# Reading back the last expert steps of a graph-and-experts kernel step by step, with the last stores on SyncE and ScalarE

## The chip, the cores and the metric

The kernel runs on one core of one Trainium2 chip. The metric is the device time of one execution in microseconds; of several executions the median is given. The core has five engines with instruction streams of their own: TensorE (PE, matmuls; PEld are its weight loads), VectorE (DVE), ScalarE (ACT), GpSimd (POOL) and SyncE (SP). Each of them runs its stream in order; SP, ACT and POOL also issue DMA transfers, which the core's 16 DMA engines carry out.

## The reference

There are 6250 nodes with 256 features and 106250 edges (100000 and a loop at each node), sorted by their destination. The kernel computes two residual parts:

```python
deg = maximum(segment_sum(ones, dst), 1);  norm = deg ** -0.5
h = (norm * (layernorm(x) @ W.T + b))[src]
x = x + segment_sum(h, dst) * norm              # graph part
z = layernorm(x)
scores = z @ Wg.T + bg                          # 8 experts
top 2 of 8, probs = softmax of the two scores
x = x + sum over the two: prob * (relu(z @ W1[e].T + b1[e]) @ W2[e].T + b2[e])
```

The hidden width of an expert is 1024. Everything is float32.

## The kernel before

Nodes lie in 49 tiles of 128 (the last has 106 real ones); tile t of the residual is kept on chip as `g.xr[:, t, :]`. The graph part gathers source rows by 831 indirect DMAs of 128 edges each (`gather`, L463, on POOL) from a table in DRAM, and sums them with 0/1 masks on TensorE (L477). The edges don't fill the last of the 831 gathers: its last 118 are padding, with source 0.

As soon as a tile of nodes is summed, its two experts are chosen and its rows are sent to one queue for each expert in DRAM (`fhq`). The expert part works in 61 steps of 256 or 128 rows (`ROWS_OF`; the last three have 128, the six before them 256). `choose(step)` takes the longest queue, as many rows as the step has place for, and notes in `at` for each node and each of its two experts in which row of the result table the answer will be. `load_first`, `load_rows` and `load_second` bring weights and rows in from SP. `up` and `down` are the pieces of TensorE work, one piece each turn. A down sum of 128 rows is in a PSUM tile `py` (two buffers); `leave` (L836) adds the bias on DVE into `y` and writes it from SP to the result table `yq` in DRAM (`fyq`). Rows 0 to 127 of `yq` are zeros. `START[step]` is the first row of a step.

Results come back to the nodes by `read_back(t, j)` (L909): one indirect gather on POOL for tile t and choice j, a row of 256 float32 into each partition of a buffer `yb` (12 buffers). `add_in` (L918) multiplies it by the node's probability and adds it to `g.xr` on DVE. Before a tile is read, `results` (L904) makes integer rows `rowat` of `at`; a row that isn't below the bound becomes row 0. The table `DONE` says after which step which tiles are complete: (55, 42) means that tiles up to 41 are complete once step 55 has left, then (57, 43), (58, 44), (59, 48), and (60, 49) at the end. `bounds` holds the same for a check at the end of the run: if a row came later than `DONE` says, a flag `g.bad` sends the program into a slower general version (`any_order`), through a branch at L1508 that every engine passes.

The order of instructions is written out by hand. In the loop from L999 each turn s emits what is due: tasks planned for this turn (`plan_at`, `in_parts`), choosing and loading, one piece of TensorE work (`next_piece`), one gather at most (L1023), one add at most (L1027, `take`, at least eight turns after its gather unless the expert steps are over or many are pending), and a store of four complete tiles from POOL. A gather is held by semaphores until the results that it reads have landed; `free_order` says that it needn't wait for later steps. After the loop (L1033 to L1053) come tile 48's rows, the check for `g.bad`, the two gathers of tile 48, the store of tiles 44 to 47 from SP and that of tile 48 from ACT.

Of the kernel before, what the change touches and what calls it, by code (L numbers as in the profile page):

```python
# [7 lines left out]
F32 = mybir.dt.float32  # L8
BF16 = mybir.dt.bfloat16
F16 = mybir.dt.float16  # L10
I32 = mybir.dt.int32
# [60 lines left out]
        (52, 41), (55, 42), (57, 43), (58, 44), (59, 48), (USUAL - 1, NT))  # L72
LATER = 1 << 17
# [75 lines left out]
def in_order(ctx: ExitStack, tc: tile.TileContext, g: Shared):  # L149
# [698 lines left out]

    tasks = {}
# [59 lines left out]
    def read_back(pool, where, t, j, upto=USUAL - 1):  # L909
# [6 lines left out]
        return t, j, yb  # L916

    def add_in(t, j, yb):  # L918
        nc.vector.scalar_tensor_tensor(g.xr[:, t, :], yb, prob[:, t, j:j + 1], g.xr[:, t, :],  # L919
                                       op0=OP.mult, op1=OP.add)  # L920
# [35 lines left out]
    with tc.manual_schedule():  # L956
# [25 lines left out]
        with tc.tile_pool(name="ftail", bufs=2) as pool:  # L982
            s = NC
            pend = []
            plan = list(DONE)
# [4 lines left out]
            def take():  # L990
                nonlocal got, stored
                t, j, yb = pend.pop(0)[1]
                add_in(t, j, yb)
                got += 1
                if got == 2 * stored + 11:
                    store(stored, stored + 4, nc.gpsimd)
                    stored += 4

            while done < USUAL or tasks or len(plan) > 1 or asked < 2 * allowed or pend:  # L999
                for fn, args in tasks.pop(s, []):  # L1000
                    fn(*args)
                if s > all_sent and s > max(STREAM)[0] + 6:
                    if chosen < min(USUAL, upped + 4):
                        run(choose(chosen))
                        chosen += 1
                    if loaded2 < min(loaded1, gone + 3):
# [10 lines left out]
                if len(plan) > 1 and done > plan[0][0] and s >= since.get(plan[0][0], 0) + 6 \  # L1017
# [8 lines left out]

                if pend and (gone == USUAL or len(pend) > 10 or s >= pend[0][0] + 8):  # L1027
                    take()
                s += 1

            results(allowed, NT, float(START[USUAL]))  # L1033
            late = work.tile([P, NT, 2], F32, name="late", bufs=1)
            missed = work.tile([P, 2], F32, name="missed")
            nc.vector.tensor_tensor(late, at, bounds, op=OP.is_ge)
            nc.vector.tensor_reduce(missed[:, 0:1], late, op=OP.add, axis=mybir.AxisListType.XY)
            nc.vector.tensor_reduce(missed[:, 1:2], most, op=OP.max, axis=mybir.AxisListType.X)
            nc.vector.tensor_scalar(missed[:, 1:2], missed[:, 1:2], float(SLOTS), None, op0=OP.is_gt)
            nc.vector.tensor_add(missed[:, 0:1], missed[:, 0:1], missed[:, 1:2])  # L1040
# [512 lines left out]
```

## Time and profile before

| | |
|---|---|
| time, median of 3 runs | 1559.64 us (1556.26 to 1563.23) |
| the profiled execution's own time | 1577.23 us |
| its span, first to last instruction | 1575.4 us |
| mean granted TensorE clock | 0.933 |
| busy: PE, DVE, POOL, ACT | 1257.4, 981.8, 905.4, 398.5 us |
| last edge gather begins (L463) | 1334.4 us |
| last piece of a down sum ends | 1553.6 us |
| last gather of results begins (L911) | 1564.7 us |
| last store issued (L928, from ACT) | 1568.8 us |

The times inside a profiled execution are those of that one execution, from its first instruction on. In the lists of the profile a line has start, duration, engine, line of the code, operation, names (written<-read), count, and in brackets how long the engine had been idle and what ended that. "issue" is time in which the engine waited for nothing that the profile shows. fyq is the result table, yb a gathered buffer, y a result on its way out.

### The profile page before, as it was taken

The numbers are of one execution on the slowest core, as the hardware profiler recorded it, in microseconds if no ns is written. First come the engines' busy times: TensorE is split into PE (matmuls) and PEld (weight loads), VectorE is DVE, ScalarE is ACT, GpSimd is POOL, SyncE is SP. The second block draws the span as 40 slices with busy tenths as digits, with TensorE's granted clock in tenths as the row PEclk, the third lists the DMA queues.
The fourth block names the chain that finished last, engine by engine and source line by source line (L and its number), as shares of the span: only waits on it lengthen the run. The fifth ranks groups of instructions, "written<-read, shape, count | busy, mean of one in ns | idle before, by whom it ended". The sixth has DMA issues, their size and how long they took to land.

```text
span 1575.4 us, 24788 instructions
## 1 busy us (share of the span) xinstructions
PE 1257.4 (80%) x6562; PEld 942.8 (60%) x6562; DVE 981.8 (62%) x5472; ACT 398.5 (25%) x949; POOL 905.4 (57%) x976
## 2 busy tenths in 40 slices
PE   5348778798889879888988887888888888867994
PEld 5225456466656656666656565666656666655773
DVE  8712665657666666776766666767756665674632
ACT  3502222122232222322222222222222222221221
POOL 3166666666566656665656656666666665236633
PEclk9968988999999989999989999999999999987997
DMA  7633385677666676766676767766767866668873
GB/s 231 208 94 90 107 289 164 187 238 231 196 209 217 209 242 214 238 196 232 209 238 186 242 193 229 213 220 219 266 219 216 273 201 222 220 209 330 292 258 119
DMA packets 160927, 337.38 MB, mean 214 GB/s; under 512 B 26900, under 2 KB 106344, under 8 KB 145160
## 3 DMA queue, kind: packets, MB, share of 16 engines
q1 hardware_dynamic: 114348, 207.57, 38.1%
q0 software_dynamic: 46176, 127.59, 28.5%
q8 instruction: 54, 0.88, 0.2%
q14 instruction: 97, 0.79, 0.2%
q10 hardware_dynamic: 252, 0.53, 0.1%
HBM read 280.44 MB, written 55.16 MB: 213 GB/s over the span
## 4 chain that ended last, share of the span: by engine, by line
PE 62%; DVE 16%; issue 9%; another core or an unknown queue 5%; DMA 4%; ACT 2%; SPq 2%; POOL 0%; ACTq 0%; DVEq 0%; POOLq 0%
PE ph L818 23%; PE py L828 18%; PE ps L477 10%; PE pt L570 3%; PE ph L520 2%; PE ps L980 2%; PE px L702 1%; PE count L295 1%; DVE mask L470 1%; SPq L725 1%; DMA w<-in_W 1%; DVE scr L754 1%; ACT hid L820 1%; DMA xT<-fhq 1%
## 5 line engine op out<-in xcount | busy, mean ns | idle before, releaser
L463 POOL DMA_INDIRECT rows<-ftable,src x831 | 789.7, 950 | 506.5 <-issue 176.5
L818 PE MATMUL ph<-xT,w 128*128 128x256 f32 (+1 forms) x1952 | 513.4, 390 | 121.1 <-issue 72.6
L818 PEld LDWEIGHTS ph<-xT,w 128*128 128x128 f32 x1952 | 363.4, 200 | 243.0 <-issue 125.2
L828 PE MATMUL py<-w,hid 128*128 128x256 f32 x1760 | 462.2, 388 | 0.8 <-ACT hid L820 0.7
L820 ACT ACTIVATE hid<-ph,w 128x256 f32<-128x256 f32 (+1 forms) x488 | 216.9, 452 | 790.2 <-PE ps L477 226.5
L828 PEld LDWEIGHTS py<-w,hid 128*128 128x128 f32 x1760 | 336.5, 194 | 77.0 <-issue 4.5
L477 PE MATMUL ps<-rows,mask 128*128 128x512 f16 x831 | 320.6, 394 | 38.4 <-DMA rows<-ftable,src 26.9
L470 DVE TENSOR_SCALAR mask<-col_b,rel 128x128 f16<-128x128 bf16 x831 | 199.5, 266 | 28.7 <-remote 18.0
L911 POOL DMA_INDIRECT yb<-fyq,rowat x98 | 95.0, 970 | 108.2 <-DMA fyq<-y 52.5
L840 DVE TENSOR_TENSOR y<-py,w 128x256 f32<-128x256 f32 x110 | 46.4, 422 | 156.2 <-PE py L828 64.2
L477 PEld LDWEIGHTS <-mask 128*128 128x128 f16 x831 | 84.7, 103 | 70.1 <-issue 26.8
L577 DVE SCALAR_TENSOR_TENSOR xr<-pt,norm,xr 128x256 f32<-128x256 f32 x49 | 23.7, 483 | 119.0 <-PE ps L477 56.1
L537 DVE SCALAR_TENSOR_TENSOR rolled<-rolled,keep,ps 128x256 f32<-128x256 f32 x149 | 70.7, 475 | 35.9 <-PE ps L477 18.7
L552 ACT ACTIVATE whole<-rolled 32x256 f32<-32x256 f32 (+2 forms) x156 | 63.9, 410 | 63.8 <-DVE rolled L537 20.4
L570 PE MATMUL pt<-gw,uT 128*128 128x264 f32 x196 | 54.9, 404 | 20.0 <-issue 11.1
L540 DVE TENSOR_TENSOR rolled<-ps,rolled 128x256 f32<-128x256 f32 x150 | 63.7, 424 | 10.4 <-DVE rolled L537 2.9
L520 PE MATMUL ph<-wg,turned 128*128 128x8 f32 x196 | 30.9, 285 | 48.2 <-ACT turned L512 36.2
L520 PEld LDWEIGHTS ph<-wg,turned 128*128 128x128 f32 x196 | 30.1, 231 | 57.1 <-ACT turned L512 41.8
L919 DVE SCALAR_TENSOR_TENSOR xr<-yb,prob,xr 128x256 f32<-128x256 f32 x98 | 46.1, 482 | 28.3 <-DMA yb<-fyq,rowat 19.1
L570 PEld LDWEIGHTS pt<-gw,uT 128*128 128x128 f32 x196 | 36.8, 194 | 34.9 <-issue 15.1
L702 PE MATMUL px<-slots,h2s 128*128 128x256 f16 x196 | 30.6, 280 | 33.0 <-DVE slots L689 10.6
L980 PE MATMUL ps<-nothing 128*128 128x512 f16 x162 | 49.8, 426 | 0.0
(187 smaller groups left out, 1152.8 us busy)
## 6 DMA issues: line engine op xcount, KB each, us to landing
w<-in_W SPq DMA_DIRECT2D x61, 1152.0 KB
w<-in_W SPq DMA_DIRECT2D x61, 1028.0 KB
fhq<-ordered SPq DMA_DIRECT2D x392, 64.0 KB
fyq<-y SPq DMA_DIRECT2D x110, 128.0 KB
rows<-ftable,src POOLq DMA_INDIRECT x831
xT<-fhq SPq DMA_DIRECT2D x49, 256.0 KB
out<-xr POOLq DMA_DIRECT2D x11, 512.0 KB
xr<-in_x SPq DMA_DIRECT2D x6, 896.0 KB
```

What stands on the lines that cost most here:

```text
L463: nc.gpsimd.indirect_dma_start(out=rows[c], out_offset=None, in_=table[:, :], in_offset=bass.IndirectOffsetOnAxis(ap=g.src[:, c:c + 1], ax ...
L470: nc.vector.tensor_scalar(masks[c], g.col_b[:, r:r + P], g.rel[:, c:c + 1], None, op0=OP.is_equal)
L477: nc.tensor.matmul(sums[w], masks.pop(c), rows.pop(c), start=(c == chunks[0]), stop=(c == chunks[-1]))
L520: nc.tensor.matmul(px[:, t - t0], xT[:, k, (t - t0) * P:(t - t0 + 1) * P], wg[:, k, :], start=(k == 0), stop=(k == 1))
L537: nc.vector.scalar_tensor_tensor(new, rolled, keeps[kept[w]], ps[:, 0:D], op0=OP.mult, op1=OP.add)
L552: nc.scalar.activation(whole[t][p0:p1, :], new[p0:p1, :], AF.Copy)
L570: nc.tensor.matmul(pl, uT[:, k, :], gw[:, k, :], start=(k == 0), stop=(k == 1))
L818: nc.tensor.matmul(ph[:, :n], w1[:, k * H + b * P:k * H + (b + 1) * P], f["xT"][:, :n, k], start=(k == 0), stop=(k == 1))
L820: nc.scalar.activation(f["hid"][:, b, :n], ph[:, :n], AF.Relu, bias=w1[:, 2 * H + b:2 * H + b + 1])
L828: nc.tensor.matmul(f["py"], f["hid"][:, b, a * P:(a + 1) * P], f["w2"][:, b * D:(b + 1) * D], start=(b == 0), stop=(b == HB - 1))
L911: r = nc.gpsimd.indirect_dma_start(out=yb, out_offset=None, in_=yq[0:START[upto + 1], :], in_offset=bass.IndirectOffsetOnAxis(ap=where[:, ...
L980: nc.tensor.matmul(sums[WINDOW[s]], nothing[:, 0:P], nothing, start=False, stop=False)
```

## The change

Tiles 42 to 48 are no longer read only when they are complete. `WHOLE` reads them, two gathers for each tile, once step 56 has left, with everything that the steps up to 56 have given. For steps 57 to 60, `own_of` works out for each node of the open tiles the row that this one step has for it (row 0 where there is none; a node has at most one row in a step) and the probability that goes with it, and `read_own` gathers it: one gather for a tile and step, for the tiles that are still open at that step (`OWN`). The adds of both kinds go through `take`. The check for `g.bad` becomes `verdict`, spread over turns after step 60 has been chosen. POOL stores tiles in fours only up to tile 39; from there stores come from ACT or SP, in the last turns. Nothing is left behind the loop.

```diff
--- before.py
+++ after.py
@@ -70,6 +70,9 @@
 
 DONE = ((36, 26), (38, 28), (40, 29), (41, 30), (42, 31), (43, 32), (46, 35), (49, 37), (50, 38), (51, 39),
         (52, 41), (55, 42), (57, 43), (58, 44), (59, 48), (USUAL - 1, NT))
+OWN = {USUAL - 1 - i: max(t for step, t in DONE if step < USUAL - 1 - i) for i in range(4)}
+SPLIT = min(OWN)
+WHOLE = [d for d in DONE if d[0] < SPLIT - 1] + [(SPLIT - 1, NT)]
 LATER = 1 << 17
 TURNED, PLACED, SORTED, SENT = 5, 17, 22, 24
 LEAD = (13, 12)
@@ -846,6 +849,57 @@
             gone += 1
 
 
+    own_row, own_share = {}, {}
+
+    def own_of(step, pool):
+
+        t0 = OWN[step]
+        lo, n = START[step], NT - t0
+        here = pool.tile([P, n, 2], F32, name="here")
+        nc.vector.tensor_scalar(here, at[:, t0:, :], float(lo + ROWS_OF[step]), None, op0=OP.is_lt)
+        nc.vector.scalar_tensor_tensor(here, at[:, t0:, :], float(lo), here, op0=OP.is_ge, op1=OP.mult)
+        yield
+        place = pool.tile([P, n, 2], F32, name="place")
+        nc.vector.tensor_mul(place, at[:, t0:, :], here)
+        own_row[step] = pool.tile([P, n], I32, name="row", bufs=4)
+        nc.vector.tensor_add(own_row[step], place[:, :, 0], place[:, :, 1])
+        yield
+        nc.vector.tensor_mul(here, here, prob[:, t0:, :])
+        own_share[step] = pool.tile([P, n], F32, name="share", bufs=4)
+        nc.vector.tensor_add(own_share[step], here[:, :, 0], here[:, :, 1])
+
+    def read_own(pool, step, t):
+        i = t - OWN[step]
+        yb = pool.tile([P, D], F32, name="yb", bufs=12)
+        r = nc.gpsimd.indirect_dma_start(
+            out=yb, out_offset=None, in_=yq[0:START[step + 1], :],
+            in_offset=bass.IndirectOffsetOnAxis(ap=own_row[step][:, i:i + 1], axis=0))
+        free_order(r, [w for of, w in writes if of > step], "rows of later steps aren't read")
+        reads.append(r)
+        return t, own_share[step][:, i:i + 1], yb, step
+
+    def verdict():
+
+        late = work.tile([P, NT, 2], F32, name="late", bufs=1)
+        missed = work.tile([P, 2], F32, name="missed")
+        nc.vector.tensor_tensor(late, at, bounds, op=OP.is_ge)
+        nc.vector.tensor_reduce(missed[:, 0:1], late, op=OP.add, axis=mybir.AxisListType.XY)
+        yield
+        nc.vector.tensor_reduce(missed[:, 1:2], most, op=OP.max, axis=mybir.AxisListType.X)
+        nc.vector.tensor_scalar(missed[:, 1:2], missed[:, 1:2], float(SLOTS), None, op0=OP.is_gt)
+        yield
+        nc.vector.tensor_add(missed[:, 0:1], missed[:, 0:1], missed[:, 1:2])
+        nc.vector.tensor_add(missed[:, 0:1], missed[:, 0:1], g.outside)
+        ones = work.tile([P, 1], F32, name="ones")
+        nc.vector.memset(ones, 1.0)
+        yield
+        yield
+        pm = psp.tile([1, 1], F32, name="pt", bufs=1)
+        nc.tensor.matmul(pm, missed[:, 0:1], ones, start=True, stop=True)
+        yield
+        yield
+        nc.vector.tensor_scalar(g.bad, pm, 1.0, None, op0=OP.min)
+
     tasks = {}
 
     def plan_at(s, fn, *args):
@@ -913,10 +967,10 @@
             in_offset=bass.IndirectOffsetOnAxis(ap=where[:, t, j:j + 1], axis=0))
         free_order(r, [w for step, w in writes if step > upto], "rows of later steps aren't read")
         reads.append(r)
-        return t, j, yb
-
-    def add_in(t, j, yb):
-        nc.vector.scalar_tensor_tensor(g.xr[:, t, :], yb, prob[:, t, j:j + 1], g.xr[:, t, :],
+        return t, prob[:, t, j:j + 1], yb, None
+
+    def add_in(t, share, yb):
+        nc.vector.scalar_tensor_tensor(g.xr[:, t, :], yb, share, g.xr[:, t, :],
                                        op0=OP.mult, op1=OP.add)
 
     def store(t0, t1, engine=None):
@@ -982,27 +1036,39 @@
         with tc.tile_pool(name="ftail", bufs=2) as pool:
             s = NC
             pend = []
-            plan = list(DONE)
+            plan = list(WHOLE)
+            own = [(step, t) for step in sorted(OWN) for t in range(OWN[step], NT)]
+            ready = OWN[SPLIT]
             got = asked = allowed = stored = 0
             latest = 0
             since = {}
 
             def take():
-                nonlocal got, stored
-                t, j, yb = pend.pop(0)[1]
-                add_in(t, j, yb)
+                nonlocal got, stored, ready
+                t, share, yb, step = pend.pop(0)[1]
+                add_in(t, share, yb)
                 got += 1
-                if got == 2 * stored + 11:
-                    store(stored, stored + 4, nc.gpsimd)
-                    stored += 4
-
-            while done < USUAL or tasks or len(plan) > 1 or asked < 2 * allowed or pend:
+                if step is None:
+                    if got == 2 * stored + 11 and stored + 4 <= OWN[SPLIT]:
+                        store(stored, stored + 4, nc.gpsimd)
+                        stored += 4
+                elif OWN.get(step + 1, NT) > t:
+                    ready += 1
+                    if t == NT - 1 or gone == USUAL and ready % 2 == 0:
+                        store(stored, t + 1, nc.scalar if t % 4 < 2 else nc.sync)
+                        stored = t + 1
+
+            while done < USUAL or tasks or plan or own or asked < 2 * allowed or pend:
                 for fn, args in tasks.pop(s, []):
                     fn(*args)
                 if s > all_sent and s > max(STREAM)[0] + 6:
                     if chosen < min(USUAL, upped + 4):
                         run(choose(chosen))
+                        if chosen in OWN:
+                            in_parts(s + 1, own_of, chosen, pool)
                         chosen += 1
+                        if chosen == USUAL:
+                            in_parts(s + 4, verdict)
                     if loaded2 < min(loaded1, gone + 3):
                         load_second(loaded2)
                         loaded2 += 1
@@ -1014,7 +1080,7 @@
                 next_piece(s)
                 if done > over:
                     since[over] = s
-                if len(plan) > 1 and done > plan[0][0] and s >= since.get(plan[0][0], 0) + 6 \
+                if plan and done > plan[0][0] and s >= since.get(plan[0][0], 0) + 6 \
                         and asked == 2 * allowed:
                     step, t1 = plan.pop(0)
                     results(allowed, t1, float(START[step + 1]))
@@ -1024,33 +1090,13 @@
                     pend.append((s, read_back(pool, rowat, asked // 2, asked % 2, latest)))
                     asked += 1
 
+                elif own and asked == 2 * NT and done > own[0][0] and s >= since[own[0][0]] + 2 \
+                        and (s % 4 or done == USUAL):
+                    pend.append((s, read_own(pool, *own.pop(0))))
+
                 if pend and (gone == USUAL or len(pend) > 10 or s >= pend[0][0] + 8):
                     take()
                 s += 1
-
-
-
-            results(allowed, NT, float(START[USUAL]))
-            late = work.tile([P, NT, 2], F32, name="late", bufs=1)
-            missed = work.tile([P, 2], F32, name="missed")
-            nc.vector.tensor_tensor(late, at, bounds, op=OP.is_ge)
-            nc.vector.tensor_reduce(missed[:, 0:1], late, op=OP.add, axis=mybir.AxisListType.XY)
-            nc.vector.tensor_reduce(missed[:, 1:2], most, op=OP.max, axis=mybir.AxisListType.X)
-            nc.vector.tensor_scalar(missed[:, 1:2], missed[:, 1:2], float(SLOTS), None, op0=OP.is_gt)
-            nc.vector.tensor_add(missed[:, 0:1], missed[:, 0:1], missed[:, 1:2])
-            nc.vector.tensor_add(missed[:, 0:1], missed[:, 0:1], g.outside)
-            ones = work.tile([P, 1], F32, name="ones")
-            nc.vector.memset(ones, 1.0)
-            pm = psp.tile([1, 1], F32, name="pt", bufs=1)
-            nc.tensor.matmul(pm, missed[:, 0:1], ones, start=True, stop=True)
-            nc.vector.tensor_scalar(g.bad, pm, 1.0, None, op0=OP.min)
-            last = [read_back(pool, rowat, t, j) for t in range(allowed, NT) for j in range(2)]
-            if stored < allowed:
-                store(stored, allowed, nc.sync)
-            for t, j, yb in last:
-                add_in(t, j, yb)
-                if j:
-                    store(t, t + 1, nc.sync if t % 2 else nc.scalar)
 
 
 @with_exitstack
```

## Prediction

> **What bounds the kernel now.** I read the page first, then the chain of waits over the last 75 us, then the timelines of POOL and DVE there, and last two narrow DMA windows for a cost that the tail of before does not show.
>
> From the page, the span, the slices of POOL and two groups:
>
> ```profile
> span 1575.4 us, 24788 instructions
> ...
> POOL 3166666666566656665656656666666665236633
> ...
> L911 POOL DMA_INDIRECT yb<-fyq,rowat x98 | 95.0, 970 | 108.2 <-DMA fyq<-y 52.5
> ...
> L919 DVE SCALAR_TENSOR_TENSOR xr<-yb,prob,xr 128x256 f32<-128x256 f32 x98 | 46.1, 482 | 28.3 <-DMA yb<-fyq,rowat 19.1
> ```
>
> TensorE bounds nearly everything up to about 1553 us, and the change leaves that part alone. What it touches is the read-back of expert results: 98 gathers on POOL, whose idle time ahead of them ended mostly with the landing of a result (fyq<-y). The last slices of POOL are loose (2, 3, 6, 6, 3, 3): it has room, but, as will be seen, not much.
>
> The end of the chain of waits (start, us, what):
>
> ```profile
> 1547.34 0.43 DVE y L840
> ...
> 1547.79 1.68 DMA fyq<-y
> ...
> 1550.23 0.95 POOL yb L911
> 1551.18 0.30 issue
> 1551.49 0.94 POOL yb L911
> ...
> 1563.44 4.25 DMA yb<-fyq,rowat
> ...
> 1568.24 0.48 DVE xr L919
> ```
>
> See how the bound changes hands. TensorE ends at 1553.5, but the chain does not run through the last step's result. It runs through step 59's (y at 1547.34), then through eight gathers one after another on POOL (tiles 44 to 47, two each), then the adds, and only then the two gathers of tile 48 and the last store. One gather costs POOL 0.95 us and 0.30 us of issue.
>
> POOL's own timeline shows the room that exists:
>
> ```profile
> 1518.03 0.80 POOL L926 DMA_DIRECT2D out<-xr  x1
> 1537.39 0.97 POOL L911 DMA_INDIRECT yb<-fyq,rowat  x1 [18.57 <-DMA fyq<-y]
> 1538.66 0.95 POOL L911 DMA_INDIRECT yb<-fyq,rowat  x1 [0.30 <-issue]
> ...
> 1556.17 0.82 POOL L926 DMA_DIRECT2D out<-xr  x1
> ...
> 1564.69 0.95 POOL L911 DMA_INDIRECT yb<-fyq,rowat  x1 [0.30 <-issue]
> ```
>
> And DVE's gives the times at which each step's result leaves:
>
> ```profile
> 1523.43 0.42 DVE L840 TENSOR_TENSOR y<-py,w 128x256 f32<-128x256 f32 x1
> ...
> 1553.61 0.42 DVE L840 TENSOR_TENSOR y<-py,w 128x256 f32<-128x256 f32 x1 [4.86 <-PE py L828]
> ```
>
> These two are the second half of step 56 and all of step 60. The last half of step 57 leaves at 1534.42, step 58 at 1539.69, step 59 at 1547.34.
>
> **The change, part by part.** *Number of gathers.* The new constants come out as SPLIT = 57 and OWN = 57:42, 58:43, 59:44, 60:48. Tiles 0 to 41 are read as before: 84 gathers. Then, once step 56 is done, tiles 42 to 48 are read for everything up to it: 7 x 2 = 14 gathers. Then step 57 is read for 7 tiles, 58 for 6, 59 for 5, 60 for one: 19. The total is 117 where it was 98. After the one store on POOL at 1518.03, before issues 14 gathers and a store; after must issue 33 gathers.
>
> *When POOL can begin.* Step 57's result left DVE at 1534.42 and its gather began at 1537.39: 2.97 us. Step 59 took 1547.34 to 1550.23: 2.89. So step 56, at 1523.43, can be gathered from about 1526.4. By the loop's counters the results row for it is asked six slots after the step ends (a slot being one piece of TensorE work, some 0.66 us here), while its landing is still under way, so the order in the program doesn't hold it back.
>
> *How long POOL needs.* The gathers from 1550.23 to 1555.23 stand 1.25 us apart; the group's mean of 970 ns with 0.30 of issue is 1.27. I take 1.26. The 33rd starts 32 x 1.26 = 40.3 us after the first: 1566.7. Before, the last started at 1564.69. The 18.57 us hole and the smaller ones (3.4, 5.0 and 2.7 us) are used up by 19 x 1.26 = 23.9 us of added work, less the store (0.82 + 0.30) that leaves POOL. Everything POOL waits for is then there already: step 57 needed 1537.4 and is asked at 1526.4 + 14 x 1.26 = 1544.0; step 58 at 1552.9 against 1542.7; step 59 at 1560.4 against 1550.2; step 60 at 1566.7 against 1556.6.
>
> *What the moved adds do to DVE.* There are 19 more adds of 0.48 us; DVE was busy 4 us between 1524 and 1550, so they fit. But DVE runs in order, and by the loop's counters the result of step 59 now stands behind 17 of the new adds, that of step 60 behind 24. The 17th gather starts at 1546.6; with 2.7 us to land (1559.82 plus 2.70 in the chain) and one add it is 1549.8, so step 59's result leaves 2.4 us late. The 24th gives 1558.6, so step 60's is 5.0 us late and can be gathered from 1561.5. POOL wants it at 1566.7: hidden, with 5 us to spare. TensorE doesn't stall on that: step 60's sum uses the PSUM buffer that step 58 freed at 1540.
>
> *Choosing rows and the verdict.* own_of adds seven small DVE operations for each of four steps, 28 x about 0.16 us (row of L763: 0.17) = 4.5 us, in parts between the pieces of steps 54 to 56. The verdict (about 1.2 us of DVE, one tiny matmul) moves from the end to the same place. DVE is busy 10.7 us of 20 between 1500 and 1520, so I take zero. Without that cover the matmul would stand in TensorE's stream waiting for DVE, at most about 1 us, and step 56 and the whole POOL chain would shift by it. The verdict was not on the old chain either: its operations ran while the last gathers flew.
>
> *Stores.* Tiles 40 to 43 leave POOL's queue and go out with 44 and 45 in one 768 KB store from ACT, then 256 KB from SP, then tile 48 from ACT. ACT's and SP's queues hold nothing else by then. Before, 512 KB stood in that place, and the gather issued just after it took 4.25 us to land against 2.70 elsewhere. I therefore give the last gather 4.25.
>
> *Rows that aren't there.* This is the cost that the tail does not show. Each partition gathers one row, and where its row is not in the step asked for it reads the zero row 0. Step 57 has at most 256 true rows over 7 x 128 reads, 58 has 128 over 768, 59 has 128 over 640: at least 640, 640 and 512 repeats, about 100 of 128 in each gather. The nearest row is the last edge gather (L463 at 1334.38): it carries the 118 padding edges, which all read row 0. Its data, beside an ordinary gather of the same 128 KB (columns: PE, PEld, DVE, ACT, POOL, clock, DMA share, GB/s):
>
> ```profile
> 1336.00:1337.70 1.70, 1.43 (x8) 0.89 (x7) 1.59 (x13) 0.47 (x1) 0.00 (x0) 1.00 0.57 77
> 1544.60:1545.40 0.80, 0.80 (x8) 0.74 (x7) 0.00 (x0) 0.25 (x1) 0.60 (x1) 1.00 0.57 164
> 25.00:26.00 1.00, 1.00 (x33) 1.00 (x33) 1.00 (x8) 0.99 (x2) 0.00 (x0) 1.00 0.34 109
> ```
>
> It took 1.7 us instead of 0.8, longer than the 1.26 at which POOL sends gathers. The third line is the bias gbs, 128 reads of one row by an ordinary DMA: 109 GB/s, which is 1.2 us per 128 KB. If gathers in a row overlap their slow ends, the engines keep pace and the backlog is 0; if each costs 1.7 us alone, it is 19 x 0.44 = 8.4 us. I take 1.5 us, nearer the lower end because ramps and slow ends of neighbours can overlap, and keep both.
>
> *A rule against the row.* The Trainium skill, "DMA: Bandwidth & Descriptors", section "Anatomy of one DMA — SWDGE (gpsimd) path", gives each POOL-issued DMA about 2.0 us fixed plus bytes / 436e3: 2.3 us for 128 KB. If each gather paid that in turn, 19 more would cost 44 us and the end would move by some 30. The trace has them 1.25 us apart while each needs about 2.7 us to land, so the fixed part overlaps with the next; I use the row.
>
> *Sum.* 1566.7 + 4.25 landing + 1.5 backlog + 0.5 for one add (before had two) = 1573.0, where before its last store was issued at 1568.75. The 6.65 us from there to the end stay. That is +4.2 us on the profiled execution of 1577.23 us (span 1575.4 and 1.8 around it). It is 1.1% above the median of 1559.64; I carry the difference over as it is: 1564.
>
> **The rivals.** *First, the gain arrives.* If POOL were not the limit, step 60's gather would start at 1556.6 and the store at 1556.6 + 3.5 + 0.5 = 1560.6, 8.1 us earlier: 1551.5. For it: behind step 60 there is one gather where there were two, and these no longer wait for the adds of tiles 44 to 47. Against it: 33 gathers between 1526.4 and 1556.6 need a pace of 0.94 us, which is the bare 0.95 without any issue time, and no pair in POOL's timeline is that close.
>
> *Second, the repeated row decides: slower.* From 1544 on the 16 DMA engines, not POOL, set the pace. Its price is 19 x 0.44 = 8.4 us in place of my 1.5, so about +11: 1571. It counts as slower from an own gather of 1.5 us upward (19 x 0.27 = 5.1 with the 2.7 of the rest gives 7.8). For it: the 1.7 us row, and that last steps may be less than full, which makes still more repeats. Against it: 109 GB/s on the broadcast load.
>
> *Third, POOL simply changes places with the wait:* the forecast itself without a backlog, +2.7: 1562.3.
>
> **How the numbers follow.** 0.5% (7.8 us) is about what a measurement of this kernel can tell from no change. The likeliest case (POOL full, backlog small) I give 0.64, within 0.5%, its own range 1558 to 1567. The repeated row deciding, with anything else that makes the new wait longer (a late verdict, the larger stores), gets 0.32 and is slower. The gain gets 0.04. The range takes the likeliest case down to 1557 (a pace of 1.2 saves 2 us, the runs shown spread by 3.5 either way) and up into the second rival: 1573.
>
> **What would show it.** Right: 117 gathers; POOL without a hole over 1 us from 1526 to the last gather; that gather starting near 1566.7 of the same clock; the chain at the end running through POOL's gathers of steps 56 to 60; step 59's and 60's y late on DVE without a TensorE stall. A gather-to-add time growing from 2.7 us to over 6 along the own gathers would show the second rival. A last gather that starts when step 60 lands, with POOL idle ahead of it, would show the first and prove me wrong; so would gathers closer than 1.2 us.

## The result and the profile after

The changed kernel took 1574.17 us (median of 6 runs, 1571.01 to 1579.58) against 1560.51 us for the kernel before (6 runs): a ratio of 1.0096, 95% interval 1.0072 to 1.0120. It is 13.7 us slower. Forecast were +4.2 us, and a range that ended at 1573.

The two profiled spans, 1575.4 and 1576.6 us, differ by 1.2 us only, because in the profiled execution of before the part up to step 56 happened to be 15 us later. Count from step 56's last y (DVE) to the end of the span instead: before 1575.4 - 1523.43 = 52.0 us, after 1576.6 - 1508.16 = 68.4 us. The tail is 16.4 us longer, and that is where the change sits. All tails below are counted like this.

The page of after (lines moved by 3 in the main part: y is now L843, the old gather L965, the new one L874):

```profile
span 1576.6 us, 24873 instructions
...
POOL 2166666666666656666666666666666663355753
...
L965 POOL DMA_INDIRECT yb<-fyq,rowat x98 | 94.5, 964 | 87.6 <-DVE mine L771 27.8
```

98 gathers as before and 19 new ones (a smaller group). POOL's last slices (5, 5, 7, 5, 3) don't tell where in the tail it stood, since one slice is 39 us long. Its timeline does (start, us, engine, line, operation, idle before and what ended it):

```profile
1511.86 0.97 POOL L965 DMA_INDIRECT yb<-fyq,rowat  x1 [7.59 <-DMA fyq<-y]
...
1535.74 0.95 POOL L874 DMA_INDIRECT yb<-fyq,row  x1 [0.30 <-issue]
1543.16 1.07 POOL L874 DMA_INDIRECT yb<-fyq,row  x1 [6.47 <-DVE xr L973]
...
1555.84 0.95 POOL L874 DMA_INDIRECT yb<-fyq,row  x1 [3.49 <-DMA fyq<-y]
...
1563.54 0.95 POOL L874 DMA_INDIRECT yb<-fyq,row  x1 [1.63 <-DVE xr L973]
```

The first 20 gathers run 1.25 us apart, as worked out. Then POOL stands: for a free buffer (an add, xr), and for step 60's result (fyq<-y). From the first of the 33 gathers to the last it is 51.7 us instead of 40.3. DVE's timeline says what came late:

```profile
1508.16 0.42 DVE L843 TENSOR_TENSOR y<-py,w 128x256 f32<-128x256 f32 x1 [1.28 <-PE py L831]
...
1521.09 0.42 DVE L843 TENSOR_TENSOR y<-py,w 128x256 f32<-128x256 f32 x1 [1.24 <-issue]
1542.07 0.42 DVE L843 TENSOR_TENSOR y<-py,w 128x256 f32<-128x256 f32 x1 [17.69 <-PE py L831]
```

These are step 56's last y, step 57's second half and step 58. In the kernel before, step 57's second half and step 58 stand so:

```profile
1534.42 0.42 DVE L840 TENSOR_TENSOR y<-py,w 128x256 f32<-128x256 f32 x1 [4.84 <-PE py L828]
1539.69 0.42 DVE L840 TENSOR_TENSOR y<-py,w 128x256 f32<-128x256 f32 x1 [4.78 <-PE py L828]
```

Step 58's y comes 21 us after step 57's second half; before, it came 5.3 us after it. DVE waited for TensorE. And the chain of waits (start, us, what) runs through TensorE, where it stands still twice:

```profile
1521.75 5.41 issue
1527.15 1.22 PE ph L821 x4
1528.37 1.71 PE py L831 x4
1530.08 9.03 issue
1539.11 1.22 PE ph L821 x4
...
1563.54 5.65 DMA yb<-fyq,row
```

"issue" means that the profile shows nothing that TensorE waited for. But each of the two matmul groups needs the PSUM buffer that a relu on ScalarE frees, and ScalarE's timeline has these just ahead:

```profile
1526.73 0.37 ACT L823 ACTIVATE hid<-ph,w 128x128 f32<-128x128 f32 x1 [7.41 <-remote]
...
1538.68 0.37 ACT L823 ACTIVATE hid<-ph,w 128x128 f32<-128x128 f32 x1 [11.58 <-remote]
```

In the kernel before, ScalarE waits about 0.95 us at this place:

```profile
1537.51 0.37 ACT L820 ACTIVATE hid<-ph,w 128x128 f32<-128x128 f32 x1 [0.90 <-PE ph L818]
```

So TensorE waits for ScalarE, and ScalarE for TensorE's signal that a sum in PSUM is complete. "remote" means that the signal arrived just then and no instruction ended near it. The matmuls in question are these:

```profile
1518.95 0.62 PE L821 MATMUL ph<-xT,w 128*128 128x128 f32 x4
...
1520.27 0.62 PE L821 MATMUL ph<-xT,w 128*128 128x128 f32 x4
```

Their ends are modelled by the profile, but the groups behind them in TensorE's order started at 1519.41 and 1520.72, and another at 1527.15. In the trace's list of semaphore updates (from which some are missing) TensorE's next counts after 1516.95 are stamped 1526.71 and 1538.61. By these starts TensorE was past the work; its signal came some 7 and 18 us after the modelled ends. The second release comes 2 us after POOL's unbroken run of gathers ends at 1536.69.

### The profile page after: what moved, and what is told of

It is laid out like the page before. It is cut to its first block, busy times and chain, and to the rows that moved or that the text cites. A ratio compares the mean times of both kernels' runs of the same rounds, so it can differ in the third digit from the quotient of the medians.

```text
span 1576.6 us, 24873 instructions
## 1 busy us (share of the span) xinstructions
PE 1258.2 (80%) x6562; PEld 946.7 (60%) x6562; DVE 988.9 (63%) x5512; ACT 399.7 (25%) x949; POOL 924.4 (59%) x994
## 4 chain that ended last, share of the span: by engine, by line
PE 31%; DVE 11%; issue 6%; another core or an unknown queue 3%; DMA 3%; SPq 1%; ACT 1%; POOL 0%; ACTq 0%; POOLq 0%; DVEq 0%
PE ph L821 12%; PE py L831 12%; PE ps L480 5%; PE pt L573 1%; DMA xT<-fhq 1%; DVE scr L757 1%; PE px L705 1%; SPq L728 1%; DVE mask L473 1%; ACT hid L823 1%; DVE xr L973 1%; DMA fhq<-ordered 0%; DVE rolled L540 0%; DVE y L843 0%
## 5 line engine op out<-in xcount | busy, mean ns | idle before, releaser
L965 POOL DMA_INDIRECT yb<-fyq,rowat x98 | 94.5, 964 | 87.6 <-DVE mine L771 27.8
L843 DVE TENSOR_TENSOR y<-py,w 128x256 f32<-128x256 f32 x110 | 46.4, 421 | 140.6 <-PE py L831 69.6
L540 DVE SCALAR_TENSOR_TENSOR rolled<-rolled,keep,ps 128x256 f32<-128x256 f32 x149 | 70.7, 474 | 28.8 <-remote 13.7
L705 PEld LDWEIGHTS <-h2s 128*128 128x128 f16 x196 | 19.8, 101 | 51.3 <-issue 41.0
```

Source lines behind the costliest of these rows:

```text
L540: nc.vector.scalar_tensor_tensor(new, rolled, keeps[kept[w]], ps[:, 0:D], op0=OP.mult, op1=OP.add)
L705: nc.tensor.matmul(r.px[:, k, :], h2s[r.t][:, i, k * P:(k + 1) * P], slots[r.t], start=(i == 0), stop=(i == 1))
L965: r = nc.gpsimd.indirect_dma_start(out=yb, out_offset=None, in_=yq[0:START[upto + 1], :], in_offset=bass.IndirectOffsetOnAxis(ap=where[:, ...
```

## Experiments

Times differ between the sessions in which kernels ran together, so each is given as a ratio to runs of the kernel before on the same chip in the same session.

### The repeated row, and the buffers

The forecast's rival was the zero row that most partitions of a new gather read. In the first run each partition's missing row is a zero row of its own (the edit in short):

```
-        own_row[step] = place[:, :, 0] + place[:, :, 1]
+        own_row[step] = max(place[:, :, 0] + place[:, :, 1], g.pid)      # the same for rowat
```

> The changed kernel, but a node that has no row in the steps asked for reads zero row p of the result table (p its partition; rows 0 to 127 are all zeros) instead of row 0: one more small DVE operation (max with the partition number) for each list of rows. As many gathers, in the same order, with the same sums. Theory A (the repeated row is what costs: gathers of one row hold the DMA engines, and ACT and TensorE stand still behind them): the 9 us and 5 us holes of TensorE after step 57 vanish or shrink below 3 us in all, the last gather is some 42 us after step 56 has left instead of 55, and the time falls from 1.0096 of before to 0.997 to 1.003. Theory B (19 more gathers on POOL and the adds queued in front of y on DVE are what costs, whatever they read): the time stays at 1.007 to 1.012.

Measured: 1599.64 against 1583.47 us, 1.0109 (1.0066 to 1.0152); tail 68.1 us. The last landing took 4.11 us instead of 5.65, but the two late signals are there as before, with ScalarE waits of 6.80 and 12.33 us. By these two profiles the repeated row costs 1.5 us once, the value taken in the forecast, and it isn't the cause of the rest.

The second variant has 24 instead of 12 buffers yb, so that POOL need not wait for adds:

```
-        yb = pool.tile([P, D], F32, name="yb", bufs=12)
+        yb = pool.tile([P, D], F32, name="yb", bufs=24)
```

> The changed kernel with 24 instead of 12 buffers yb, so that POOL doesn't wait for adds that stand behind a late y on DVE (its hole of 6.5 us). If the chain POOL waits for DVE waits for TensorE is what lengthens the end, POOL's hole goes and the time falls by about 6 us (to about 1.006 of before); if DMA is what limits (theory A), gathers are issued earlier but land no earlier: within 0.2% of the changed kernel's 1.0096.

Measured: 1610.40 us, 1.0177 (1.0133 to 1.0220), worse than the change itself. The tail, 70.3 us, is no shorter: POOL's run now has 21 gathers and ends at 1569.38, and ScalarE is free at 1573.16. The rest of the loss lies ahead of the tail, since the edit gives the earlier gathers more buffers too: from the first gather of results to step 56's last y it is 174.1 us, where the run before this one took 164.5, and POOL's longest unbroken run there has 27 DMAs instead of 22. The lack of buffers is not what holds the kernel up. It only ends POOL's run earlier.

### Gathers that nobody reads, in the kernel before

Nineteen gathers more in the kernel before, after step 57, in three turns of four, into buffers that nothing reads. In the first all partitions read row 0, in the second partition p reads row p:

```
+            more, spare = 19, pool.tile([P, 1], I32, name="spare", bufs=1)
+            nc.vector.tensor_scalar(spare, g.pid, 0.0, None, op0=OP.mult)      # 1.0 in the second
...
+                if more and done > 57 and s % 4:
+                    nothing_back = pool.tile([P, D], F32, name="nb", bufs=12)
+                    nc.gpsimd.indirect_dma_start(out=nothing_back, ..., in_=yq[0:P, :], in_offset=spare)
+                    more -= 1
```

> The kernel before with 19 gathers more, emitted from the turn after step 57 on, three turns in four; all 128 partitions read row 0, into buffers that nothing reads. They wait for no result, so POOL has room for most of them in the hole that it had from 1518 to 1537. Theory A: they slow the landing of weights, results and rows around them; stands of ACT and TensorE appear while they fly, and the time rises by 0.5% or more (8 us and up). Theory B: POOL only fills its hole, a few of the 19 push the gathers of tiles 42 to 47 back by 0 to 6 us; the time rises by at most 0.3%, the same as with 19 different rows.

> As the run with 19 gathers of row 0 more, but partition p reads row p: the same number, size and places, no repeats. Theory A: near the time of before (0.998 to 1.003), and clearly below the run with repeats. Theory B: the same time as the run with repeats.

Measured: 1.0103 (1.0059 to 1.0146) and 1.0086 (1.0053 to 1.0119); tails of 71.0 and 67.6 us. Neither the adds nor the choosing of rows nor the stores of the change are in these kernels, and a cost of the same size is there. ScalarE's waits in the tail of the second (us in total, times, longest):

```profile
ACT hid L820 <- remote: 18.0, 3, 7.4
```

### What it is about a gather

Four ways to have a part of a gather. POOL busy without any transfer (19 memsets of the same length); the transfers without POOL (19 plain loads of 128 KB from SP); gathers of a quarter of the data; and full gathers scattered over steps 41 on.

```
+                    nothing_set = pool.tile([P, 1250], F16, name="nb", bufs=2)       # POOL alone
+                    nc.gpsimd.memset(nothing_set, 0.0)
...
+                    nc.sync.dma_start(nothing_back, yq[0:P, :])                      # transfers alone
...
+                    nc.gpsimd.indirect_dma_start(out=nothing_back[:, 0:64], ...)     # rows of 256 bytes
...
+                if more and done > 40 and s % 16 == 0:                               # scattered
```

> Part changed: 19 memsets of a 128x1250 f16 tile that nobody reads (by the 0.51 us of the 128x512 memset some 1.25 us each, the pace of the gathers) stand on POOL where the run of 19 cold gathers stood, after step 57; no transfer is added. In the runs with 19 idle gathers TensorE and ScalarE stood still in steps 58 to 60 and the time rose by 14 to 16 us; in the traces ScalarE's unexplained waits lie inside unbroken stretches of POOL's gathers and end 1.5 to 2 us after the stretch ends. Theory P (a POOL that is occupied without a break holds the other engines up): +10 us or more, with ScalarE waits of 4 us and more put down to 'remote'. Theory T (it is the gathers' transfers or their descriptors): within 3 us of before, or up to 10 us more where POOL's own 14 gathers are pushed back by memsets not yet done, with no such ScalarE waits.

> Part changed: before with 19 plain loads of 128 KB (128 rows of 1 KB, like a gather's) from SP's queue in the same turns after step 57, into buffers that nobody reads. The bytes and the row size are those of the 19 gathers, POOL has nothing more to do. Theory T-bytes (the traffic holds ScalarE and TensorE up): +10 us or more with ScalarE waits put down to 'remote' in steps 58 to 60. Theory P or a theory in which POOL's own descriptor work counts: within 3 us of before, or a few us more from y stores standing behind the loads in SP's queue.

> Part changed: before with 19 gathers of 128 rows of 256 bytes (64 columns, a quarter of the data) in the same turns after step 57, into buffers that nobody reads. Descriptors and POOL's work are those of the 1 KB gathers. If POOL's descriptor work counts: +14 to 16 us as with full rows. If the bytes count: a quarter, +3 to 5 us. If it is neither and only the place in the schedule: the same as the full rows.

> Part changed: before with the 19 cold gathers of full rows one by one, a turn in sixteen from step 41 on (some 10 us apart by emission), instead of in a bunch after step 57. If it is the unbroken stretch of gathers that holds ScalarE up: within 4 us of before, as each lengthens a stretch by 1.25 us at most. If every gather more costs some 0.8 us wherever it stands: +14 to 16 us.

Measured against 1580.57 us: POOL alone 1.0038 (1.0019 to 1.0057), transfers alone 1.0010 (0.9987 to 1.0033), narrow gathers 1.0102 (1.0065 to 1.0139), scattered 1.0084 (1.0052 to 1.0116).

The memsets' 6 us are another thing: they push POOL's own last gathers back, and ScalarE waits for nothing unexplained. Its waits in that tail:

```profile
ACT hid L820 <- PE ph L818: 17.5, 20, 1.3
ACT hid L820 <- issue: 0.4, 1, 0.4
```

With plain loads there is no "remote" in the tail either. With a quarter of the data it is all there:

```profile
ACT hid L820 <- remote: 18.5, 4, 8.8
```

So it is neither the bytes, nor a busy POOL, nor a plain transfer from SP: it comes with POOL's indirect DMAs, and as strongly with small rows. Plain DMAs issued by POOL in such a run were not tried.

The scattered gathers went against the expectation that the run was written for: no gain from spreading. The trace tells why. Its tail is undisturbed (53.4 us, no late signal), but before step 56 POOL already issues gathers in long runs, and the scattered ones lengthened these; one unbroken run of POOL's DMAs goes from 1509.96 to 1533.97. ScalarE's late signals from the first gather of results on:

```profile
ACT hid L820 <- remote: 64.9, 13, 10.9
```

With the plain loads, in the same session, they were 35.2 us there.

### Runs cut by pauses, and another engine for the relu

Two theories were left. G: a long unbroken run of gathers holds TensorE's signals up until about 2 us after its end. C: each gather costs so much wherever it stands. The changed kernel, with a POOL memset of 2.2 us after every fourth of the last 33 gathers:

```
+                        asked_late += 1
+                        if asked_late % 4 == 0:
+                            nothing_set = pool.tile([P, 2500], F16, name="nb", bufs=2)
+                            nc.gpsimd.memset(nothing_set, 0.0)
```

> Part changed: the changed kernel, in which POOL runs a memset of a 128x2500 f16 tile that nobody reads (some 2.3 us) after every fourth of its last 33 gathers, so that no run of gathers is longer than 5 us. Theory G (gathers in an unbroken run hold ScalarE up from about the sixth on, until 2 us after the run's end): the ScalarE waits of 7 and 12 us in steps 58 and 59 go, and from step 56's last y to step 60's y it is 30 to 35 us as in the kernel before, not 50; the time is then set by POOL (33 gathers of 1.25 and 8 memsets of 2.3 us, some 60 us after step 56's y, with landing and store 68): about the time of the changed kernel, 0 to +5 us. Theory C (each gather more costs TensorE's chain some 0.75 us wherever it stands): step 60's y still comes 50 us after step 56's, and the time is 10 us or more above the changed kernel's.

Measured: 1.0120 (1.0076 to 1.0164) against 1561.28 us; tail 73.4 us. Of ScalarE's waits none in the tail is "remote", and TensorE ends its last matmul 30.1 us after step 56's y, as in the kernel before. Yet step 60's y is late, as C had it, and for a reason that neither theory had. DVE's timeline (steps 58, 59, 60) and waits:

```profile
1531.51 0.42 DVE L843 TENSOR_TENSOR y<-py,w 128x256 f32<-128x256 f32 x1
...
1546.86 0.42 DVE L843 TENSOR_TENSOR y<-py,w 128x256 f32<-128x256 f32 x1
...
1559.28 0.41 DVE L843 TENSOR_TENSOR y<-py,w 128x256 f32<-128x256 f32 x1
```

```profile
DVE xr L973 <- DMA yb<-fyq,row: 26.7, 19, 3.3
```

With POOL slowed down, the adds that stand ahead of y in DVE's order wait for their gathers, and y behind them. That is the forecast's "What the moved adds do to DVE", larger, and here it is the pauses that make it so.

The other run takes the kernel before with the 19 unread gathers, and moves the relu of steps 58 to 60 to DVE:

```
+        if step > 57:
+            nc.vector.tensor_scalar(f["hid"][:, b, :n], ph[:, :n], w1[:, 2 * H + b:2 * H + b + 1], 0.0,
+                                    op0=OP.add, op1=OP.max)
+            return
```

> Part changed: before with the 19 cold gathers after step 57 (as in the run that cost 14 us), and the relu of steps 58 to 60 on VectorE instead of ScalarE. If only ScalarE is held up while gathers run: TensorE doesn't stand still in steps 58 to 60, step 60's y comes some 30 us after step 56's, and of the +14 us 6 or so are left (POOL's own gathers pushed back, as the memsets showed). If whatever engine waits for TensorE is held up: VectorE waits take the place of ScalarE's, and +14 us stays.

Measured: 1.0085 (1.0049 to 1.0120), nothing gained. The late signals follow to the new engine; DVE's waits:

```profile
DVE hid L821 <- remote: 8.4, 2, 4.5
...
DVE y L844 <- remote: 3.8, 1, 3.8
```

It isn't ScalarE that is held up, but whoever waits for TensorE.

### Less of the change

Only the last step, or the last two, read by themselves:

```
-OWN = {...  for i in range(4)}
+OWN = {...  for i in range(1)}      # 99 gathers; range(2): 104
```

> Part changed: the changed kernel with only the last step read back by itself (one tile, 99 gathers in all instead of 117): the results of steps up to 59 are gathered two a tile for all tiles after step 59, and one gather waits for step 60. Theory G and theory C alike: no run of gathers over 6 us before step 60's relus are done and one gather more than before, so no stall of ScalarE in steps 58 to 60; after step 60's y one gather is left instead of two, and the last one starts some 2 us earlier: -1 to -3 us against before. If the moved verdict or the last stores cost something: at or above before.

> Part changed: the changed kernel with the last two steps read back by themselves (104 gathers instead of 117): 12 gathers follow step 58's y, 5 step 59's, 1 step 60's. Theory G: a run of 12 gathers from step 58's y on lies beside steps 59 and 60, of which the last 6 or so hold ScalarE up for 4 to 10 us: +2 to +8 us against before. Theory C: 6 gathers more at 0.75 us: +4 us. If gathers cost nothing beyond POOL's time: 0 to -3 us.

Measured: 1.0005 (0.9984 to 1.0026) and 1.0026 (1.0003 to 1.0049), with no "remote" wait in the tail of the first; in the second ScalarE has 3.6 us of them, and DVE's wait before step 60's y is one of 10.7 us. The small change alone is no gain: its last gather, of mostly repeated rows, took 4.85 us to land. But it is no loss, so the moved verdict and the new last stores, which both kernels have, cost nothing that can be measured.

### Breaks in the kernel before

If long runs hold TensorE up, the kernel before should gain from breaks, for it has long runs too. Its ScalarE timeline has three late signals in a row, and all lie inside one run of POOL's from 1420.65 to 1447.22:

```profile
1436.13 0.47 ACT L820 ACTIVATE hid<-ph,w 128x256 f32<-128x256 f32 x1 [3.82 <-remote]
1440.42 0.47 ACT L820 ACTIVATE hid<-ph,w 128x256 f32<-128x256 f32 x1 [3.81 <-remote]
1445.44 0.47 ACT L820 ACTIVATE hid<-ph,w 128x256 f32<-128x256 f32 x1 [4.55 <-remote]
```

A memset on POOL after every fifth gather up to step 57, of 2.2 us or of 0.95 us, in the kernel before; and the long ones in the one-step change:

```
+                    if asked % 5 == 0 and done < 58:
+                        nothing_set = pool.tile([P, 2500], F16, name="nb", bufs=2)       # or 1000
+                        nc.gpsimd.memset(nothing_set, 0.0)
```

> Part changed: the kernel before, in which POOL runs a memset of a 128x2500 f16 tile that nobody reads (2.2 us) after every fifth gather of results as long as step 57 is not done; gathers, order and transfers are those of before. In the trace of before ScalarE waits some 38 us in all for signals of TensorE between 1364 and 1500 us, inside POOL's runs of 10 to 20 gathers. Theory G (a long unbroken run holds the signals up): most of these waits go, and the time falls by 8 to 20 us, as TensorE sets the pace there; POOL becomes some 35 us busier, of which its idle stretches of 19 us and more before step 57's landing take most. Theory C (a cost per gather, not per run): the waits stay, and the time is that of before or up to 10 us more.

> Part changed: the same with memsets of 128x1000 f16 (some 0.9 us). Theory G with a hold that lasts until 1.5 to 2 us after a run's last gather: a break of 1.1 us in all is too short to end it, or ends it only in part: between before and the run with long breaks, 0 to -8 us. If any break at all ends a run: as with the long ones, -8 to -20 us. Theory C: as before or some us more.

> Part changed: the changed kernel with only the last step read back by itself (99 gathers), and a memset of 128x2500 f16 after every fifth gather as long as step 57 is not done. Theory G: as the kernel before with the same breaks, within 3 us: -8 to -20 us against before. Theory C: 0 to +10 us.

Measured against 1559.89 us: long breaks 0.9964 (0.9930 to 0.9997), short breaks 0.9855 (0.9803 to 0.9907), the one-step change with long breaks 1.0031 (1.0013 to 1.0049). Adding nothing but 16 memsets of 0.95 us makes the kernel before 21 us faster. The breaks stand only in the part from the first gather of results on. ScalarE's late signals there, in the profiles of before, with short breaks and with long ones:

```profile
ACT hid L820 <- remote: 40.2, 9, 11.0
...
ACT hid L820 <- remote: 21.0, 6, 4.7
...
ACT hid L820 <- remote: 3.6, 2, 3.2
```

From the first gather of results to step 56's last y these three profiles take 159.2, 142.5 and 159.0 us, so the gain of the short breaks lies where they stand.

I had expected the short breaks to do less than the long ones. For the late signals that is so: the short ones halve them, the long ones remove nearly all. But the time goes the other way, because the long ones slow the gathers. With them, up to step 56's last y, DVE's adds wait for gathers and TensorE waits for a y behind such adds:

```profile
DVE xr L919 <- DMA yb<-fyq,rowat: 42.9, 29, 5.9
...
PE py L828 <- DVE y L840: 14.2, 3, 5.3
```

In before the first is 9.7 us and the second is absent; with short breaks they are 30.9 and 4.1 us. Why the one-step change with long breaks stands 0.7% above the kernel before with them, when without breaks the two are level, no run settles.

### The change with short breaks

The whole change with a memset of 0.95 us after every fifth of all its gathers; the one-step change with them; and the kernel before with memsets of 128x250 (0.33 us).

```
+                    if asked % 5 == 0:            # and after every fifth of the own gathers
+                        nothing_set = pool.tile([P, 1000], F16, name="nb", bufs=2)
+                        nc.gpsimd.memset(nothing_set, 0.0)
```

> Part changed: the changed kernel with a memset of 128x1000 f16 (0.95 us) on POOL after every fifth of its 117 gathers, the last 33 too. If the hold-up was all that the prediction missed: the stall of 7 and 12 us in steps 58 and 59 goes; from step 56's last y to the end it is the kernel before's 52 us, plus the forecast's 4, plus 6 breaks of 1.1 us: some 63 us instead of 68, and with the 21 us that the breaks saved in steps 36 to 57 some 1550 us, -10 us against before and 11 us above the kernel before with the same breaks. If VectorE's late adds hold the y of steps 58 to 60 back as well (as in the run with breaks of 2.2 us): 66 to 70 us, 1553 to 1557 us.

> Part changed: the change for the last step only (99 gathers) with a memset of 128x1000 f16 after every fifth gather as long as step 57 is not done. The small change alone stood at 1.0005 of before, so with these breaks it should stand where the kernel before does with them: 0.985 of before, -20 to -24 us. If the long breaks' difference between the two (0.9964 and 1.0031) was the small change's own: 0.99, some 10 us above.

> Part changed: the kernel before with a memset of 128x250 f16 (some 0.25 us) on POOL after every fifth gather of results as long as step 57 is not done. If any break of POOL's gathers ends a run: -15 to -25 us, as with 0.9 us or a little more for the time saved on POOL. If the signals need about a microsecond without a gather: 0 to -10 us, with ScalarE waits put down to 'remote' of 3 us and more left in place.

Measured: 1.0197 (1.0172 to 1.0223), 1.0099 (1.0082 to 1.0116), 1.0014 (0.9998 to 1.0030). These ratios can't be set beside the earlier ones, since beside these three the kernel before took 1311.13 us, some 250 us less than in the other sessions; the same chip had given 1561.28 in an earlier one. The traces show what was absent: in all three, not one wait of any engine is "remote", though POOL goes from one DMA to the next with hardly a gap. TensorE's granted clock was also higher (0.975 in the third run, 0.933 in the profile of before). Most of the 250 us lie ahead of the read-back: the last edge gather begins at 1118.61 in the third run and at 1334.38 in the profile of before. From 80 us on up to there TensorE is idle for 50 us of 1038 in the one and 218 of 1254 in the other; how much of that is late signals isn't worked out. The breaks had no late signals to remove here and only cost, 13 us in the one-step change.

But for the prediction this is the best run of all: the change without the hold-up. POOL's timeline, first and last of the 33 gathers:

```profile
1274.97 0.97 POOL L965 DMA_INDIRECT yb<-fyq,rowat  x1 [9.61 <-DMA fyq<-y]
...
1320.48 0.94 POOL L874 DMA_INDIRECT yb<-fyq,row  x1 [0.32 <-issue]
```

Between them no hole is over 0.32 us. The tail is 1334.4 - 1271.22 = 63.2 us, where the expectation had worked out 63. That close a match is partly luck, since it took a break at 1.1 us: a gather behind a break starts 2.07 us after the one ahead of it instead of 1.25, so a break costs 0.82. Taking off 6 of them leaves an estimate of 58.3; the forecast's tail was 52.0 + 4.2 = 56.2. So without late signals the forecast is met within some 2 us, and the change would still lose a little.

## Why the prediction was wrong, step by step

- *Number of gathers*: right, 117, and 33 of them in a row.
- *When POOL can begin*: 2.97 us after step 56's y forecast, 3.7 measured.
- *How long POOL needs*: this step failed. The pace of 1.25 us was right, but "everything POOL waits for is then there already" was not. POOL stood for 12 us, and the last gather came 51.7 instead of 40.3 us after the first. This is 11.4 of the 12.2 us by which the tail missed the forecast (68.4 against 56.2).
- *What the moved adds do to DVE*: "TensorE doesn't stall on that" failed, though not by the adds. The forecast put the effect of POOL's run on TensorE and ScalarE at nothing. TensorE stood for 14.4 us because its own signals were late while POOL ran its gathers. The kernels with unread gathers show it with no add moved. From there the loss went in a circle: step 58's y late, the adds behind it late, no free buffer, POOL stands, and only then the signals come through. That the adds would delay y itself was right in kind: without the hold-up step 60's y came 42.8 us after step 56's, where TensorE had ended after 30.1, and POOL did not wait for it. The size was 12.7 us, with the breaks in it, where 5.0 was forecast.
- *Choosing rows and the verdict*: taken as zero, and small. The verdict's matmul waited 0.9 us for DVE, the "at most about 1 us" that the forecast gave for the case without cover; it lies ahead of the tail.
- *Stores* and *rows that aren't there*: right. The last gather landed in 5.65 us, forecast 4.25 + 1.5; with distinct rows it was 4.11.
- *The rivals*: the repeated row as the pace-setter fell with the first run. That its +11 us came nearest to the measured 13.7 is an accident. The gain couldn't arrive: POOL's time for 33 gathers exceeds what the last steps take, with or without the hold-up.
- *Direction*: the forecast held "no measurable difference" likeliest. Its sum was short by one term, the hold-up. A sign of it stood in the trace of before: 107.7 us of "remote" waits ahead of ScalarE's relus. Their places alone prove little. Of the 19 over 2.5 us, 6 end inside an unbroken run of POOL's DMAs and 13 end 0.1 to 2.5 us after one, but POOL is in or just behind such a run for most of the time anyway. It took the unread gathers and the breaks to show the link.

What stays open is what on the chip delays the signals, and why it was absent in one session. Shown is that it comes with POOL's indirect DMAs in a row, doesn't depend on their bytes, hits ScalarE and DVE alike when they wait for TensorE, and is cut by breaks on POOL, by half with 0.95 us and nearly wholly with 2.2 us. How short a break suffices wasn't told apart, since the shortest ran where nothing was held up. Nor is a long run always needed: 67.5 of the 107.7 us lie ahead of the read-back, where most of POOL's runs of edge gathers have only 4 to 7. All executions listed have spans and clocks from the profiler, so no run shows whether the signals are late without it.

## What to carry to other kernels

Before filling an engine's idle time with work that "hides", look at what the other engines do while that engine is full now: unexplained waits of the others may be a cost that the added work will pay again. A wait that the profile can't put down to an instruction is worth an experiment before it is taken for noise; a table against an engine's busy stretches says little when that engine is busy most of the time. And when a loss shows, undo it by parts that nothing reads: 19 idle gathers, idle memsets and idle loads told within a few runs what reasoning about the change's own dependencies had wrong.

## What the hardware showed unexpectedly

- TensorE's completion signals can arrive 3 to 18 us late while POOL issues indirect DMAs 1.25 us apart. In the tails of the change, its variants with other zero rows or 24 buffers, and the unread gathers (distinct rows, small rows), the late ones begin 6 to 8 us into a run and the last comes 2.0 to 3.8 us after its end. With 19 memsets on POOL, or 19 plain 128 KB loads from SP, the tail had none.
- A break of 0.95 us after every fifth gather was worth 21 us (0.9855) to a kernel that had been tuned, with no other edit; in the session without late signals the same breaks gained nothing: with the one-step change the kernel was 13 us above before (1.0099).
- The kernel before took 1311 us in one session and 1560 to 1583 us in the others; every profile of the slower sessions has late signals, none of the faster one has. Chip and program were the same in one pair of these sessions.
- The last gather, of mostly one row, took 5.65 us to land; with distinct rows it took 4.11 (one profile each).
